# A graph layer's edge sort: the bucket numbers of a comparison are read from PSUM, beside the counts

## The chip, the core and the metric

The kernel runs on one core of a Trainium2 chip. The metric is the device time of one launch in microseconds (us). The engines are named as in the profile: PE (matrix products; PEld is its loading of weights), DVE (vector operations), ACT (activations and copies), POOL (here the issue of indirect DMAs), SP (the queue of most plain DMAs).

## What is computed

A residual graph layer over 12500 nodes of 64 features and 212500 edges (100000 drawn pairs in both directions and one loop for each node). The edges are sorted by `dst`, and `src` is the node that the sums go to.

```python
h = jnp.maximum(_layernorm(x, axis=-1), 0.0)
edge_in = jnp.concatenate([h[row], h[col], dist], axis=1)     # row = src, col = dst
e = jax.nn.silu(edge_in @ eW1 + eb1)
e = jax.nn.silu(e @ eW2 + eb2)
agg = jax.ops.segment_sum(e, row, num_segments=h.shape[0])
node_in = jnp.concatenate([h, agg], axis=1)
out = jax.nn.silu(node_in @ nW1 + nb1) @ nW2 + nb2
x + out
```

## The kernel before

Node `n` belongs to bucket `n mod 100` (`NB` = 100 buckets of `L` = 125 nodes). The kernel writes each edge's half-finished row (the part of the first layer that comes from `dst` and from the distance, 128 numbers, and 16 copies of the edge's place in its bucket) into a table `q` in DRAM, into the bucket of its `src`, at a rank that it counts itself. Then it reads buckets back and finishes the edges there: the `src` part, SiLU, the second product, SiLU, and a product with a 0/1 matrix that sums by node into `aggT`. A last part computes the nodes' output.

*The sorting half* goes by blocks of 1024 edges (`BLK`), 208 blocks, each as 8 tiles of 128 edges (`TB` = 8). `count(s)` finds the ranks of block `s` in three steps, each up to a `yield`:

- On DVE, `oh` (line 352) compares the numbers 1 to 100 with the bucket numbers of the block's edges, `buckets`, a slice of `bkE`: 8 x 100 results on each partition. `each` (line 360) sums `oh` over the 8 tiles. For every second block, `pick` (line 364) builds the selection matrix of the pair of blocks.
- On PE, two products add to the running counts `full`, which stay in PSUM through all blocks: `rest` with the `each` of the block before (line 369), then `before` with the `each` of this block (line 387). Where a level of buckets closes, DVE reads `full` between them (`u`, line 380, and a few more).
- On DVE, `mine` (line 402) multiplies `oh` with `full`, `rank` (line 404) sums it, and `to` (line 406) makes the row numbers. `to` has four buffers.

`send(s)` multiplies the `pick` of a block with its window of rows (PE, `qp`, line 427), copies the results to `qs` (ACT, lines 437 and 443; eight buffers), and issues eight indirect DMAs from POOL (line 450), one for each tile of 128 edges. Each scatters 128 rows of 144 numbers to the rows of `q` that a column of `to` names. `send_all` runs `send(s)` beside `count(s + 1)`, step by step, so on PE the `qp` products of a block stand ahead of the two counting products of the next block, which stand together.

*The finishing half* goes by batches of a level and four buckets, in 450 steps of four tiles: `lr`, `oneT`, `pt`, `e1`, `one`, `p2`, `e2`, `seg`, `aggT` (lines 526 to 603). Its inputs are `qt`, a stretch of `q`, and `a`. It starts while the sorting half still runs: a level of buckets can be read as soon as all edges that can fall into it have been sent.

The order of the work on PE, DVE, ACT and SP is the order in which the program is written (the kernel sets it by hand). A list `turn` gives the order of the finishing steps, with four places in it at which a piece of the sorting half goes in; `marks` says how many pieces must have gone by each step. The semaphores are set by the framework from the tiles that instructions read and write.

In PSUM the pool `sg` holds `full` and the sums `seg` of a batch; the pool `mm` holds four tiles that all other products share, and `p2` two.

Of the kernel before, what the change touches and what calls it, by code (L numbers as in the profile page):

```python
# [28 lines left out]
F32 = mybir.dt.float32  # L29
# [9 lines left out]
P = 128  # L39
# [9 lines left out]
TB = BLK // P  # L49
# [24 lines left out]
def tile_gnn(ctx: ExitStack, tc: tile.TileContext, x, src, dst, ew, eW1, eb1, eW2, eb2, nW1, nb1, nW2, nb2, out):  # L74
    nc = tc.nc
# [4 lines left out]
    NB = N // L  # L80
# [61 lines left out]
    nodes1 = const.tile([P, L], F32, name="nodes1")  # L142
# [126 lines left out]
    with ExitStack() as work:  # L269
        mm = work.enter_context(tc.tile_pool(name="mm", bufs=4, space=PSUM))  # L270
        p2p = work.enter_context(tc.tile_pool(name="p2", bufs=2, space=PSUM))
        sgp = work.enter_context(tc.tile_pool(name="sg", bufs=1, space=PSUM))
# [2 lines left out]
                engines={mybir.EngineType.PE, mybir.EngineType.DVE, mybir.EngineType.Activation, mybir.EngineType.SP}  # L275
            )
        )
        full = sgp.tile([P, NB], F32, name="full")
        nc.tensor.matmul(full, before, identb[:, :NB], start=True, stop=True)
        nc.vector.memset(full, -1.0)  # L280
        mine = cnt.tile([P, TB, NB], F32, name="mine")
        sums = []
        blk, lists = {}, {}
# [43 lines left out]
        def weights(s):  # L327

            if s < nblocks:
                p, g = s // 2, s % 2  # L330
                pick = lists[p][1][:, g]
                e0 = s * BLK
                m = 1 if p == 0 or e0 + 2 * BLK > E else 2
                if m == 2 or e0 + BLK <= E:
                    of = bass.AP(tensor=ew.tensor, offset=ew.offset + e0, ap=[[QR, NQR], [BLK, m], [1, QR]])
                    nc.sync.dma_start(lists[p][1][WL::32, g : g + m, :], of)
                else:
                    for a in range(NQR):
                        m = min(QR, E - e0 - a * QR)
                        if m > 0:  # L340
                            of = bass.AP(tensor=ew.tensor, offset=ew.offset + e0 + a * QR, ap=[[m, 1], [1, m]])
                            nc.sync.dma_start(pick[a * 32 + WL : a * 32 + WL + 1, :m], of)

        def count(s):

            if s < nblocks:
                bc, win, pick = blk[s]
                p, g = s // 2, s % 2
                whole = p > 0 and (2 * p + 2) * BLK <= E
                buckets = bkE[:, g * TB : (g + 1) * TB, p]  # L350
                oh = wk.tile([P, TB, NB], BF16, name="oh")
                nc.vector.tensor_tensor(  # L352
                    oh,
                    nodes1[:, None, :NB].to_broadcast([P, TB, NB]),
                    buckets[:, :, None].to_broadcast([P, TB, NB]),
                    op=OP.is_equal,
                )
                each = wk.tile([P, NB], BF16, name="each")
                with nc.allow_low_precision("whole numbers up to eight"):
                    nc.vector.tensor_reduce(each, oh.rearrange("p t b -> p b t"), AX.X, OP.add)  # L360
                if not whole:
                    nc.vector.tensor_scalar(pick, bc, same, plus, op0=OP.is_equal, op1=OP.add)
                elif g == 0:
                    nc.vector.tensor_scalar(lists[p][1], lists[p][0], same, plus, op0=OP.is_equal, op1=OP.add)
            yield
            if s < nblocks and (g == 0 or not whole):
                weights(s)
            if s > 0:
                nc.tensor.matmul(full, rest, sums.pop(), start=False, stop=True, skip_group_check=True)
            limits = [(SURE[w], OP.is_gt) for w in ready_at if s == ready_at[w]]  # L370
            closed = s > 0 and (s == nblocks or needed[s] != needed[s - 1])
            if closed:
                limits.append((SURE[needed[s - 1]], OP.is_lt))
            if s == nblocks:
                limits.append((ROWS, OP.is_gt))
            if limits:
                u = wk.tile([P, NB], F32, name="u")
                v = wk.tile([P, 1], F32, name="v")
            for limit, op in limits:
                nc.vector.tensor_scalar(u, full, float(G * limit - 1), None, op0=op)  # L380
                nc.vector.tensor_reduce(v, u, AX.X, OP.max)
                nc.vector.tensor_tensor(bad[:, 1:2], bad[:, 1:2], v, op=OP.add)
            if s == nblocks:
                return
            if closed and LEVELS[needed[s - 1]][2]:
                nc.vector.tensor_scalar(full, full, float(G * ENDS[needed[s - 1]] - 1), None, op0=OP.max)
            nc.tensor.matmul(full, before, each, start=False, stop=True, skip_group_check=True)  # L387
            sums.append(each)
            if g == 0:
                assert p in scaled  # L390
                both = bkE[:, :, p].rearrange("p (g t) -> p g t", g=2)
                wide = [P, 2, TB, TB]
                eq = wk.tile(wide, F32, name="eq")
                nc.vector.tensor_tensor(
                    eq, both[:, :, :, None].to_broadcast(wide), both[:, :, None, :].to_broadcast(wide), op=OP.is_equal
                )
                nc.vector.tensor_tensor(eq, eq, early[:, None].to_broadcast(wide), op=OP.mult)
                pre = wk.tile([P, 2 * TB], F32, name="pre")
                nc.vector.tensor_reduce(pre.rearrange("p (g t) -> p g t", g=2), eq, AX.X, OP.add)
                nc.vector.tensor_tensor(offE[:, :, p], offE[:, :, p], pre, op=OP.add)  # L400
            yield
            nc.vector.tensor_tensor(mine, oh, full[:, None, :].to_broadcast([P, TB, NB]), op=OP.mult)  # L402
            rank = wk.tile([P, TB], F32, name="rank")
            nc.vector.tensor_reduce(rank, mine, AX.X, OP.add)  # L404
            to = top.tile([P, TB], I32, name="to")
            nc.vector.scalar_tensor_tensor(  # L406
                to, rank, float(G * ROWS - 1), offE[:, g * TB : (g + 1) * TB, p], op0=OP.min, op1=OP.add
            )
            blk[s].append(to)
            yield  # L410
# [60 lines left out]
        def send_all(s0, s1):  # L471

            for s in range(s0, s1):
                load(s + 2)
                i, rest = divmod(s - FILL0, FILL_EACH)
                if rest == 0 and 0 <= i < len(fills):
                    fill(*fills[i])

                for j, _ in enumerate(itertools.zip_longest(send(s), count(s + 1))):
                    pending[needed[s]] -= j == PIECES - 1  # L480
                    yield
# [329 lines left out]
        with tc.tile_pool(name="lists", bufs=1, side="right") as lp:  # L811
# [40 lines left out]
            list(scale(0, FIRST))  # L852
            load(0)
            counting = count(0)
            next(counting)
            todo = groups()
# [214 lines left out]
```

## Time and profile before

| what | value |
|---|---|
| median of 3 runs | 2500.06 us (2492.88 to 2503.01) |
| profiled execution, its own time | 2495.92 us |
| its span in the trace | 2494.1 us |
| mean granted PE clock | 0.915 |
| PE, DVE, POOL, ACT busy | 82%, 78%, 70%, 44% |
| indirect DMAs of POOL, line 450 | 1661, mean 1030 ns |
| `oh`, line 352 | 208, mean 984 ns |

The page gives the busy time of each engine, the span in 40 slices, the DMA queues, the chain of work that ended last, and the costliest groups of instructions. A group's line has the line of the kernel, the engine, the operation, what it writes and reads, how often it ran, its busy time and mean, and then the idle time of its engine just before it with what ended that idle time. Other views give the waits between engines, the instructions of one line, and the instructions in order of time. Releasers are inferred, and a wait is put down to what came last.

### The profile page before, as it was taken

Reading aid. Unit: us, or ns where it says so; the run is one execution under the profiler, and the core shown is the slowest. Engines: PE = TensorE matmul, PEld = TensorE weight load, DVE = VectorE, ACT = ScalarE, POOL = GpSimd, SP = SyncE. Lnnn points to the kernel's source line nnn. Section 1 sums busy time; section 2 is a strip of 40 time slices with the busy share of each in tenths; the row PEclk is TensorE's granted clock in tenths of the full one; section 3 lists DMA queues with packets and bytes.
Section 4 is the critical chain, followed back from the end, with each engine's and each line's share of the span. In section 5 each row is a group of like instructions: output and inputs, shape, how many; then the busy total and the mean of one; then the engine's idle time right before and its main releaser. Section 6 shows DMA issues by size and latency. Waiting matters only on the chain.

```text
span 2494.1 us, 46291 instructions
## 1 busy us (share of the span) xinstructions
PE 2056.3 (82%) x16191; PEld 1838.5 (74%) x16191; DVE 1936.9 (78%) x3005; ACT 1088.6 (44%) x2403; POOL 1740.7 (70%) x1712
## 2 busy tenths in 40 slices
PE   3663776655588888998889998899999999999997
PEld 2552665555577777887878887788888899999986
DVE  7885677666788887888878888888888899986532
ACT  2451333322244444544444444455455555554442
POOL 4677777777777777777777777777777777762110
PEclk9575888877899998999999999999999999999999
DMA  4563556555667765676645554555555556665652
GB/s 118 182 213 119 168 183 188 179 166 176 194 198 223 222 198 169 219 222 206 202 152 165 164 164 150 165 165 178 166 168 173 179 167 201 216 205 171 194 164 66
DMA packets 237007, 443.85 MB, mean 178 GB/s; under 512 B 49805, under 2 KB 108736, under 8 KB 236562
## 3 DMA queue, kind: packets, MB, share of 16 engines
q1 hardware_dynamic: 158629, 269.79, 35.4%
q0 software_dynamic: 53536, 123.03, 14.2%
q10 hardware_dynamic: 24602, 47.98, 6.6%
q8 instruction: 132, 2.16, 0.4%
q14 instruction: 108, 0.88, 0.1%
HBM read 251.07 MB, written 189.55 MB: 177 GB/s over the span
## 4 chain that ended last, share of the span: by engine, by line
PE 39%; DMA 17%; POOL 14%; DVE 13%; issue 8%; ACT 2%; SPq 0%; DVEq 0%; POOLq 0%; ACTq 0%
DMA q<-qs,to 15%; POOL q L450 14%; PE seg L592 9%; PE pt L546 8%; PE p L578 7%; PE pt L540 4%; PE qp L427 4%; PE lr L526 2%; DVE oh L352 2%; DVE oneT L531 2%; DVE each L360 2%; DVE one L559 2%; DVE aggT L603 2%; DMA qt<-q 1%; DVE mine L402 1%
## 5 line engine op out<-in xcount | busy, mean ns | idle before, releaser
L450 POOL DMA_INDIRECT q<-qs,to x1661 | 1711.6, 1030 | 586.1 <-issue 402.2
L550 ACT ACTIVATE e<-pt 128x512 f32<-128x512 f32 x450 | 268.7, 597 | 867.4 <-PE pt L546 865.2
L592 PE MATMUL seg<-one,e 128*128 128x125 f32 x3600 | 510.3, 287 | 119.0 <-DVE aggT L603 83.7
L592 PEld LDWEIGHTS seg<-one,e 128*128 128x128 f32 x3600 | 462.1, 201 | 170.0 <-issue 110.8
L578 PEld LDWEIGHTS p<-w,e 128*128 128x128 f32 x3600 | 472.0, 196 | 54.2 <-issue 37.3
L546 PE MATMUL pt<-oneT,a 125*128 125x128 f32 (+1 forms) x2400 | 486.8, 337 | 20.0 <-DVE oneT L531 20.0
L578 PE MATMUL p<-w,e 128*128 128x128 f32 x3600 | 494.1, 281 | 0.0
L546 PEld LDWEIGHTS pt<-oneT,a 125*128 125x128 f32 x2400 | 366.3, 199 | 40.6 <-DVE oneT L531 23.1
L437 ACT COPY qs<-qp 128x512 f32<-128x512 f32 x416 | 224.7, 588 | 370.9 <-PE qp L427 321.9
L531 DVE TENSOR_SCALAR oneT<-lr,part 125x512 f32<-125x512 f32 x450 | 335.0, 745 | 48.8 <-PE lr L526 46.8
L360 DVE TENSOR_REDUCE each<-oh 128x100 bf16<-128x800 bf16 x208 | 315.8, 1518 | 7.2
L559 DVE TENSOR_TENSOR one<-nodes,qt 128x500 f32<-128x500 f32 x450 | 302.3, 672 | 0.0
L540 PE MATMUL pt<-ident,qt 128*128 128x128 f32 x1800 | 288.3, 285 | 1.3 <-DVE oneT L531 1.3
L427 PE MATMUL qp<-win,pick 64*128 64x256 f32 x1662 | 270.5, 440 | 22.5 <-DMA win<-tb 6.1
L582 ACT ACTIVATE e<-p 128x512 f32<-128x512 f32 x450 | 268.6, 597 | 27.9 <-PE p L578 27.6
L572 ACT COPY p<-b2f 128x512 f32<-128x512 f32 x450 | 267.2, 594 | 0.0
L406 DVE SCALAR_TENSOR_TENSOR to<-rank,offE 128x8 int32<-128x8 f32 x208 | 36.2, 174 | 280.0 <-DMA q<-qs,to 274.8
L427 PEld LDWEIGHTS qp<-win,pick 64*128 64x128 f32 x1662 | 165.4, 206 | 98.5 <-issue 63.0
L540 PEld LDWEIGHTS pt<-ident,qt 128*128 128x128 f32 x1800 | 201.8, 148 | 48.7 <-issue 38.8
L603 DVE TENSOR_TENSOR aggT<-aggT,seg 128x500 f32<-128x500 f32 x275 | 184.0, 669 | 67.8 <-PE seg L592 64.3
L404 DVE TENSOR_REDUCE rank<-mine 128x8 f32<-128x800 f32 x208 | 205.1, 986 | 7.2
L402 DVE TENSOR_TENSOR mine<-oh,full 128x800 f32<-128x800 bf16 x208 | 203.8, 980 | 6.8 <-PE full L387 6.6
(144 smaller groups left out, 1457.0 us busy)
## 6 DMA issues: line engine op xcount, KB each, us to landing
qt<-q SPq DMA_DIRECT2D x150, 576.0 KB
a<-ta SPq DMA_DIRECT2D x300, 256.0 KB
qt<-q SPq DMA_DIRECT2D x150, 288.0 KB
q<-zeros ACTq DMA_DIRECT2D x25, 1080.0 KB
q<-qs,to POOLq DMA_INDIRECT x1661
q<-zeros ACTq DMA_DIRECT2D x10, 1440.0 KB
bc<-dests SPq DMA_DIRECT2D x103, 128.0 KB
win<-tb SPq DMA_DIRECT2D x416, 30.0 KB
```

The costliest lines, as they stand in the source:

```text
L360: nc.vector.tensor_reduce(each, oh.rearrange("p t b -> p b t"), AX.X, OP.add)
L427: nc.tensor.matmul(qps[i][:, t, : n_of[t]], pick[at, t * P : (t + 1) * P], win[at, : n_of[t]], start=True, stop=True)
L450: ins = nc.gpsimd.indirect_dma_start(out=q[:], out_offset=bass.IndirectOffsetOnAxis(ap=to[:k, j : j + 1], axis=0), in_=qs[:k, t, a, :], in ...
L531: nc.vector.tensor_scalar(oneT, st[k].pop("lr")[:L], part1[:L, :], None, op0=OP.is_equal)
L540: nc.tensor.matmul(pt[:, t, :], qt[:, j, :H], ident, is_transpose=True, start=t == 0, stop=False, skip_group_check=True)
L546: nc.tensor.matmul(pt[:, cols, :], a[:L, b, :], oneT[:, cols, :], start=False, stop=True, skip_group_check=True)
L550: nc.scalar.activation(e1, pt, AF.Silu)
L559: nc.vector.tensor_tensor(one.rearrange("p (b j) l -> p b j l", j=n), nodes1[:, None, None, :].to_broadcast(wide), loc[:, tiles[0][1] : ti ...
L572: nc.scalar.copy(p2, b2f)
L578: nc.tensor.matmul(p2[:, t, :], e1[:, t, :], w2, start=False, stop=t == G - 1, skip_group_check=True)
L582: nc.scalar.activation(e2, p2, AF.Silu)
L592: nc.tensor.matmul(item[2][:, b, :], e2[:, t, :], one[:, t, :], start=j < G, stop=j >= G * (n - 1))
```

## The change

The PSUM tile `full` becomes the first 100 columns of a tile `counts` of 200 columns, in the same pool and one bank. A DVE copy writes the numbers 1 to 100 into the other 100 columns, once, before the first block. `oh` reads these numbers as its first input in place of `nodes1` in SBUF; its second input, `buckets`, stays in SBUF, and its output stays bf16 in SBUF. `nodes1` itself stays, since `one` and the set-up read it.

```diff
-        full = sgp.tile([P, NB], F32, name="full")
+        counts = sgp.tile([P, 2 * NB], F32, name="counts")
+        full, numbers = counts[:, :NB], counts[:, NB:]
         nc.tensor.matmul(full, before, identb[:, :NB], start=True, stop=True)
         nc.vector.memset(full, -1.0)
+        nc.vector.tensor_copy(numbers, nodes1[:, :NB])
         mine = cnt.tile([P, TB, NB], F32, name="mine")
...
                 oh = wk.tile([P, TB, NB], BF16, name="oh")
                 nc.vector.tensor_tensor(
                     oh,
-                    nodes1[:, None, :NB].to_broadcast([P, TB, NB]),
+                    numbers[:, None, :].to_broadcast([P, TB, NB]),
                     buckets[:, :, None].to_broadcast([P, TB, NB]),
                     op=OP.is_equal,
                 )
```

In the built program the order of instructions is the same on every engine, but for the new copy and its neighbour in the set-up on DVE.

## Prediction

> **What bounds the kernel now.** I read the page first (busy times, the chain), then the scatter's own line with its waits, then a stretch of the timeline, then a table of stretches. The page's engine totals mislead: PE is busiest over the span, yet for most of it nothing waits for PE alone.
>
> ```profile
> PE 2056.3 (82%) x16191; PEld 1838.5 (74%) x16191; DVE 1936.9 (78%) x3005; ACT 1088.6 (44%) x2403; POOL 1740.7 (70%) x1712
> ...
> PE 39%; DMA 17%; POOL 14%; DVE 13%; issue 8%; ACT 2%; SPq 0%; DVEq 0%; POOLq 0%; ACTq 0%
> DMA q<-qs,to 15%; POOL q L450 14%; PE seg L592 9%; PE pt L546 8%; PE p L578 7%; PE pt L540 4%; PE qp L427 4%; PE lr L526 2%; DVE oh L352 2%; DVE oneT L531 2%; DVE each L360 2%; DVE one L559 2%; DVE aggT L603 2%; DMA qt<-q 1%; DVE mine L402 1%
> ```
>
> The chain is split between PE and the indirect scatters of POOL (line 450), with their landings. Now line 450 alone: its durations, what POOL waited for, and who waited for it.
>
> ```profile
> L450 POOL DMA_INDIRECT q<-qs,to x1661: 898/967/2278, 39.3 to 2314.1; - x185
> ...
>   issue: 402.2, 1317
> ...
>   DVE to L406: 274.8, 92
>   ACT qs L437: 48.9, 16
> ```
>
> Between 100 and 2240 us of the trace this line is busy 1649.5 us and idle before itself 489.4 us: 2138.9 of 2140. The idle part is a fixed 0.305 us ahead of each of its 1603 scatters; whatever name stands on such a gap, its length is the same. So POOL is full for 2140 us, and DVE waits for it (274.8 us at `to`, whose four buffers are still being scattered). The rows show `to` ready 25 to 30 us ahead of the block's first scatter in nearly all of it. In this stretch the time is POOL's time, one scatter every 0.967 + 0.305 = 1.272 us plus what lengthens some of them.
>
> What lengthens them is in the timeline:
>
> ```profile
> 1200.11 0.98 DVE L352 TENSOR_TENSOR oh<-nodes,bkE 128x800 bf16<-128x800 f32 x1
> ...
> 1200.51 1.43 POOL L450 DMA_INDIRECT q<-qs,to  x1 [0.30 <-issue]
> ...
> 1204.39 0.97 DVE L402 TENSOR_TENSOR mine<-oh,full 128x800 f32<-128x800 bf16 x1
> ...
> 1204.79 0.97 POOL L450 DMA_INDIRECT q<-qs,to  x1 [0.30 <-issue]
> ```
>
> Both scatters start 0.40 us into a DVE instruction of 800 elements. Under `oh`, whose two inputs are both in SBUF, the scatter takes 1.43 us and ends 0.84 us after `oh` does; under `mine`, with `full` in PSUM, it takes its usual 0.97. All rows say the same: of the scatters that reach their 0.13th us inside an `oh`, 128 of 142 are lengthened; inside `one` (two SBUF inputs) 110 of 136; inside `mine` 2 of 150; inside `oneT` (from PSUM) 0 of 249; inside `aggT` (one PSUM input) 0 of 79. The lengthening is 105 us in all; scatters that end 0.84 us after an `oh` carry 54.8 us of it (124 scatters), after a `one` 33.3 us (123), after an `eq` 6.9 us (47).
>
> Last, where POOL stops being the only bound:
>
> ```profile
> 1600.00:2000.00 400.00, 375.79 (x3057) 340.34 (x3056) 348.68 (x527) 204.15 (x436) 308.24 (x302) 0.99 0.53 172
> 2000.00:2240.00 240.00, 233.99 (x2121) 220.89 (x2120) 219.06 (x339) 125.33 (x264) 183.90 (x178) 1.00 0.64 199
> 2240.00:2494.00 254.00, 237.28 (x2028) 216.78 (x2026) 117.16 (x197) 104.72 (x213) 38.65 (x46) 0.98 0.49 150
> ```
>
> Columns: stretch, length, busy PE, PEld, DVE, ACT, POOL, clock, DMA share, GB/s. PE is at 94% up to 2000 us, 97.5% up to 2240, and alone after that.
>
> **The change, part by part.** *Set-up*: a DVE copy of 100 elements joins once; the like-sized `u` took 258 ns. Before the first scatter at 39.3 us DVE is a chain, so 0 to 0.3 us; I take 0.2.
>
> *DVE time of `oh`*: 208 instructions of 984 ns. With one input in PSUM the nearest rows are `mine`, same 800 elements, 980 ns, and `aggT` from PSUM, 669 ns, beside `one` from SBUF, 672 ns, both of 500. So 208 x (-4 to 0 ns) = -0.8 to 0 us, off the path while DVE waits for POOL: 0. [...]
>
> *The wait on the counts' bank*: since `oh` now reads the tile that PE's counting products write, the product with `rest` (line 369) waits for the `oh` of the block; in the built program's order 176 of these 208 products carry a DVE wait, against 49 before. Behind it on PE stand the product with `before`, then the `pt`, `p`, `seg` of the running batch. But the very next product, with `before`, already waits for `each` (141.4 us over 45 waits), which DVE runs directly after `oh` for 1.52 us. The `rest` product takes 0.22 us and lies wholly inside that: nothing is later. The cover is gone only if `each` ended less than 0.22 us after `oh`; then a block would pay up to 0.22 + 0.33 us (the issue gap seen ahead of line 369), 208 x 0.55 = 114 us of PE, of which only the 23 blocks after 2000 us, 13 us, are on the path. In the other direction `oh` carries no wait for PE, since the `mine` ahead of it on DVE has already waited for the same product. DVE's order is otherwise unchanged. I take 0, range 0 to 13.
>
> *POOL*: with the numbers in PSUM, `oh` has one SBUF input left, as `mine` has, and its 54.8 us go. Part comes back: a scatter held by `oh` restarts in step with DVE, and so misses the next `one` more often. Compare blocks: the 122 with a scatter held by `oh` lose 128 ns to other instructions, the 78 without lose 376. If every block went over to the second kind, 122 x 0.248 = 30 us would return, the upper bound; the lower is 0. For a value I walked along the recorded DVE rows with one scatter every 1.272 us, held when it starts more than 0.02 us after the start of a two-SBUF instruction and over 0.13 us before its end. The walk, restarted at each block's recorded scatter, gives 55 for `oh`, 35 for `one`, 96 in all, near the rows' 54.8, 33.3 and 105; with `oh` struck out `one` costs 47 and the sum is 53. So 12 us return, and POOL's stretch gets 43 us shorter (25 to 55).
>
> *Who is late next*: PE. Before 2000 us lie 88% of the stretch, 38 us; PE's 94% there becomes 96%, under the 97.5% that it reaches later, so I let them through. After 2000 PE has 6 us idle in 240; of the 5 us due there I count 1. The tail after 2240 us is PE's alone: 0. Sum: 38 + 1 - 0.2 = 39 us. The profiled execution was 2495.92 us (span 2494.1), so 2457 for its like; it lies 4 us under the median of 2500.06, and from the median it is 2461.
>
> **Rivals.** *The order of operands decides.* `oh` reads PSUM as its first input and SBUF (`buckets`) as its second; `mine` and `aggT` have it the other way round, and no row shows this order while POOL scatters. If the second input is what shuts POOL out, nothing changes: 2500, 2495 to 2505. That is the case in which the change does not do what it says. For it speaks only this gap; against it, that all rows with one PSUM input are clean. [...]
>
> *Freed, but taken up.* The upper give-back (30 us) together with a PE that cannot go past its 94% before 2000 us: 55 - 30 = 25 us of which the 20% that lie after 1600 us are lost, 20 us; with `eq` caught more too, 5 to 20. Time 2480 to 2495. For: PE is at 94% there. Against: 97.5% a little later.
>
> [...]
>
> **How the numbers follow.** The forecast 0.73, range 2443 (all 55 us) to 2478; freed but taken up 0.10; no change 0.12; slower 0.05. About 0.5%, 12.5 us, is what a measurement of this kernel can tell from no change. The forecast is wholly past that; the second case mostly (0.07 of its 0.10). Faster 0.80, same 0.15, slower 0.05. The range for 8 in 10 runs from 2443 to 2492, taking in nearly all of the first two cases.
>
> **What would show it.** Right: the scatters that end 0.84 us after an `oh` are gone, line 450's mean falls from 1030 ns to about 1004, `one` holds more than now, POOL's last scatter comes near 2275 instead of 2315 us, the waits of `to` on scatters shrink, PE between 1600 and 2000 us rises past 95%. Wrong: scatters of 1.4 us under `oh` still there (operand order), PE waits at line 369's successor with DVE long done (the bank), or an `oh` over 1.02 us.

## Result and the profile after

The changed kernel took 2463.94 us in the median of 4 runs (2459.37 to 2467.58), the kernel before 2499.5 us in its 4. The ratio is 0.986 with a 95% interval of 0.9832 to 0.9888: 36 us, or 1.4%, faster. The profiled execution took 2461.70 us (span 2459.9).

First the page after: the busy times and the chain.

```profile
PE 2045.2 (83%) x16191; PEld 1829.8 (74%) x16191; DVE 1936.9 (79%) x3006; ACT 1088.8 (44%) x2403; POOL 1705.5 (69%) x1712
...
PE 36%; DMA 17%; DVE 16%; POOL 13%; issue 8%; ACT 2%; DVEq 0%; POOLq 0%; ACTq 0%; SPq 0%
```

DVE is as busy as before to 0.1 us; POOL is busy 35 us less for the same 1661 scatters. Now the groups of instructions: the scatter's line, and the two counting products on PE. First before, then after.

```profile
L450 POOL DMA_INDIRECT q<-qs,to x1661 | 1711.6, 1030 | 586.1 <-issue 402.2 <-ACT qs L443 84.0 <-DMA q<-qs,to 42.4
...
L369 PE MATMUL full<-each,rest 128*128 128x100 bf16 x208 | 46.6, 224 | 0.6 <-DVE mine L402 0.6
L387 PE MATMUL full<-each,before 128*128 128x100 bf16 x208 | 45.4, 218 | 174.0 <-DVE each L360 141.4 <-DVE u L380 22.2 <-DVE full L386 10.3
```

```profile
L452 POOL DMA_INDIRECT q<-qs,to x1661 | 1676.4, 1009 | 586.3 <-issue 396.9 <-ACT qs L445 85.4 <-DMA q<-qs,to 43.7
...
L371 PE MATMUL counts<-each,rest 128*128 128x100 bf16 x208 | 46.5, 224 | 92.0 <-DVE oh L354 92.0
L389 PE MATMUL counts<-each,before 128*128 128x100 bf16 x208 | 45.1, 217 | 73.2 <-DVE each L362 48.8 <-DVE u L382 13.9 <-DVE counts L388 10.2
```

The mean scatter went from 1030 to 1009 ns (the prediction's sign was about 1004), while the idle time ahead of the scatters stayed (586.1 and 586.3 us). The new wait is there, 92.0 us at the product with `rest`, and the old one at the product with `before` has shrunk to 73.2; before, they were 0.6 and 174.0.

The timeline after has a scatter that starts 0.38 us into an `oh`, and a little later one that starts 0.41 us into a `one`.

```profile
369.20 0.98 DVE L354 TENSOR_TENSOR oh<-counts,bkE 128x800 bf16<-128x800 f32 x1
369.58 0.97 POOL L452 DMA_INDIRECT q<-qs,to  x1 [0.31 <-issue]
...
374.52 0.67 DVE L561 TENSOR_TENSOR one<-nodes,qt 128x500 f32<-128x500 f32 x1
374.93 1.11 POOL L452 DMA_INDIRECT q<-qs,to  x1 [0.31 <-issue]
```

Under `oh` the scatter now takes its usual 0.97 us; under `one`, still with two inputs in SBUF, it is held and takes 1.11. Over all rows: scatters that start inside an `oh` (0.02 us after its start to 0.15 us before its end) were held in 124 cases of 125 before, and in 0 of 114 now.

Last, the stretches that answer to those of before (length, busy PE, PEld, DVE, ACT, POOL, clock, DMA share, GB/s).

```profile
1600.00:1970.00 370.00, 352.45 (x2906) 320.39 (x2905) 327.93 (x500) 194.53 (x416) 284.28 (x282) 1.00 0.54 175
1970.00:2205.00 235.00, 229.45 (x2081) 216.73 (x2080) 215.04 (x331) 122.05 (x257) 178.74 (x175) 1.00 0.65 198
2205.00:2460.00 255.00, 237.85 (x2032) 217.31 (x2031) 117.43 (x198) 105.18 (x213) 38.66 (x46) 0.98 0.50 150
```

PE went from 94% to 95.3% in the first stretch and from 97.5% to 97.6% in the second. POOL is full up to about 2210 us now instead of 2245; the stretch behind it is as long as it was.

### The profile page after: what moved, and what is told of

It is laid out like the page before. It is cut to its first block, busy times and chain, and to the rows that moved or that the text cites. A ratio compares the mean times of both kernels' runs of the same rounds, so it can differ in the third digit from the quotient of the medians.

```text
span 2459.9 us, 46292 instructions
## 1 busy us (share of the span) xinstructions
PE 2045.2 (83%) x16191; PEld 1829.8 (74%) x16191; DVE 1936.9 (79%) x3006; ACT 1088.8 (44%) x2403; POOL 1705.5 (69%) x1712
## 4 chain that ended last, share of the span: by engine, by line
PE 36%; DMA 17%; DVE 16%; POOL 13%; issue 8%; ACT 2%; DVEq 0%; POOLq 0%; ACTq 0%; SPq 0%
DMA q<-qs,to 16%; POOL q L452 13%; PE seg L594 8%; PE pt L548 8%; PE p L580 7%; PE pt L542 4%; PE qp L429 4%; DVE oh L354 2%; DVE each L362 2%; DVE oneT L533 2%; PE lr L528 2%; DVE aggT L605 2%; DVE one L561 2%; DVE mine L404 1%; DVE rank L406 1%
## 5 line engine op out<-in xcount | busy, mean ns | idle before, releaser
L452 POOL DMA_INDIRECT q<-qs,to x1661 | 1676.4, 1009 | 586.3 <-issue 396.9
L594 PE MATMUL seg<-one,e 128*128 128x125 f32 x3600 | 504.0, 285 | 110.2 <-DVE aggT L605 77.7
L594 PEld LDWEIGHTS seg<-one,e 128*128 128x128 f32 x3600 | 456.0, 199 | 140.0 <-issue 84.7
L404 DVE TENSOR_TENSOR mine<-oh,counts 128x800 f32<-128x800 bf16 x208 | 203.9, 980 | 8.3 <-PE counts L389 8.0
```

Of the source, the lines that this page charges most:

```text
L452: ins = nc.gpsimd.indirect_dma_start(out=q[:], out_offset=bass.IndirectOffsetOnAxis(ap=to[:k, j : j + 1], axis=0), in_=qs[:k, t, a, :], in ...
L594: nc.tensor.matmul(item[2][:, b, :], e2[:, t, :], one[:, t, :], start=j < G, stop=j >= G * (n - 1))
```

## Experiments

The theory: POOL's scatters set the time; a scatter that starts inside a DVE instruction with two SBUF inputs is held (inside `oh` before, 124 of 125), so that it ends 0.84 us after that instruction does; the change takes `oh` off that list, and the time falls by what the scatters then lose less. The rivals were the order of the operands, a price of the new wait, and a PE that takes the gain up. All results stand together first. "Lengthened" is the time of all scatters over 0.968 us each, "idle" what POOL idled between scatters over the fixed 0.306 us, both from the rows of the profiled execution; "rest" is the span less the end of the last scatter.

Each ratio is against runs of the kernel before made beside that kernel (their medians were 2499.5 us for the second row, 2497.4 for the next four, 2496.7 for the last two), so it is not quite the quotient of the medians shown.

| kernel | median us | ratio to before | lengthened | of it `oh` / `mine` / `one` | idle | last scatter ends | rest |
|---|---|---|---|---|---|---|---|
| before | 2499.5 | 1 | 106.0 | 54.8 / 0 / 33.3 | 58.0 | 2315.0 | 179.1 |
| changed | 2463.9 | 0.986 | 71.0 | 0 / 0 / 46.5 | 58.1 | 2280.2 | 179.7 |
| inputs of `oh` exchanged | 2464.1 | 0.9863 | 72.5 | 0 / 0 / 46.7 | 59.8 | 2283.2 | 179.2 |
| wait alone | 2499.8 | 1.0003 | 109.3 | 50.0 / 0 / 41.3 | 61.1 | 2321.4 | 179.6 |
| `oh` and `one` from PSUM | 2421.7 | 0.9695 | 15.4 | 0 / 0 / 0 | 74.4 | 2240.2 | 178.8 |
| `mine` from an SBUF copy | 2551.4 | 1.0226 | 130.4 | 0 / 54.1 / 56.7 | 86.8 | 2367.9 | 178.8 |
| copy, `mine` from PSUM | 2518.5 | 1.0097 | 67.4 | 0 / 0 / 43.6 | 119.0 | 2336.9 | 178.8 |
| `one` alone from PSUM | 2468.2 | 0.9895 | 68.3 | 54.8 / 0 / 0 | 68.2 | 2287.0 | 178.8 |

Take "lengthened" and "idle" from the end of the last scatter and 2150 to 2151 us are left in all eight kernels. That by itself is bookkeeping: 1661 scatters of 0.968 us, 1660 gaps of 0.306 us and a first scatter at 39 us make 2155, less some 4 us of scatters and gaps that are a little shorter. What the runs add is that the 179 us behind the last scatter stay, so that the time moves with two sums alone: the lengthening and POOL's idle time. A kernel wins only what it takes off the first and does not add to the second.

**The order of the inputs.** The changed kernel, with the two inputs of `oh` exchanged.

```diff
-                    numbers[:, None, :].to_broadcast([P, TB, NB]),
                     buckets[:, :, None].to_broadcast([P, TB, NB]),
+                    numbers[:, None, :].to_broadcast([P, TB, NB]),
```

> Theory (what shuts POOL out is the number of inputs in SBUF, not their order): with the two inputs of oh exchanged, bucket numbers first from SBUF and the numbers 1 to 100 second from PSUM, the time stays at that of the changed kernel, 2464 us within 6, and no scatter ends 0.84 us after an oh; PSUM as the first input was clean in the changed kernel, PSUM as the second was clean in mine. Rival (some of the gain hangs on PSUM being first): scatters held by oh come back, up to 55 us of them, and the time goes to 2475 to 2500.

Ratio 0.9863 (0.9844 to 0.9883), and 0 of the 106 scatters that start inside an `oh` are held. With PSUM as the first input (0 of 114) as with PSUM as the second, `oh` leaves the scatters alone. This rival falls, by the changed kernel itself and by this one.

**The wait alone.** The kernel before, with the product with `rest` waiting for `oh`.

```diff
-                nc.vector.tensor_tensor(
+                compared = nc.vector.tensor_tensor(
...
-                nc.tensor.matmul(full, rest, sums.pop(), start=False, stop=True, skip_group_check=True)
+                ins = nc.tensor.matmul(full, rest, sums.pop(), start=False, stop=True, skip_group_check=True).ins
+                if s < nblocks:
+                    tc.add_manual_dep(ins, compared.ins.name, AFTER)
```

> The kernel before, with one thing of the change alone: the product with rest waits for the oh of its block, as it does in the changed kernel; the numbers stay in SBUF. Theory (the wait lies inside the wait for each that follows): 2500 us within 5, the idle time of PE moves from the product with before to the product with rest and their sum stays near 164 us (174 us of PE idle before line 387 now, 10 of it at a closing level). Rival (the product with rest now comes after the wait and PE pays 0.22 to 0.55 us a block): 13 us or more above the kernel before, 2513 to 2525, and the changed kernel would have won as much more without the wait.

Ratio 1.0003 (0.9993 to 1.0012, 11 runs): at most 3 us. The groups of this kernel:

```profile
L369 PE MATMUL full<-each,rest 128*128 128x100 bf16 x208 | 47.2, 227 | 99.5 <-DVE oh L352 99.5
L389 PE MATMUL full<-each,before 128*128 128x100 bf16 x208 | 45.5, 219 | 76.0 <-DVE each L360 52.5 <-DVE u L382 12.7 <-DVE full L388 10.5
```

99.5 and 76.0 us make 175.5, against 0.6 and 174.0 before: the idle time moved from one product to the other. The wait costs nothing here, because the second product has to wait for `each` anyway.

**More of the same.** The changed kernel, with the numbers 1 to 125 for `one` in the same bank.

```diff
-        counts = sgp.tile([P, 2 * NB], F32, name="counts")
-        full, numbers = counts[:, :NB], counts[:, NB:]
+        counts = sgp.tile([P, NB + L], F32, name="counts")
+        full, numbers, all_numbers = counts[:, :NB], counts[:, NB : 2 * NB], counts[:, NB:]
...
-        nc.vector.tensor_copy(numbers, nodes1[:, :NB])
+        nc.vector.tensor_copy(all_numbers, nodes1)
...
-                nodes1[:, None, None, :].to_broadcast(wide),
+                all_numbers[:, None, None, :].to_broadcast(wide),
```

> The changed kernel, with the numbers 1 to 125 of one in the bank of the counts too. Theory (POOL's scatters are the bound until PE is): the 46 us that scatters lose to one go, 5 to 15 of them come back at eq and pick, POOL's last scatter is 30 to 40 us earlier, at 2240 to 2250; PE, at 96% from 1600 us on, lets 10 to 30 us of it through: 2434 to 2454. Rival (PE has become the bound, and one now waits for the counting product and the counting product for one): POOL's scatters run 0.97 us each but wait, the time is 2460 to 2490.

2421.7 us, ratio 0.9695 (0.9679 to 0.971): the fastest kernel of the study, 76 us under the kernel before of the same runs. The last scatter came where it was expected, at 2240 us, though not by the steps expected, and the time beat the expected range. Nothing came back at `eq` and `pick`: the lengthening fell by 55.6 us, 46.5 of them at `one`. Against that POOL idled 16.3 us more, most of it from 2112 us on, and it waited for `qs` 99.8 us instead of 85.4. So about 16 of the 56 us were taken up by POOL's waits, and the other 40 came off the end. PE was busy 96.6% of the time between 1600 and 2150 us. It idled longer at the product with `rest`, which now waits for `one` too (141.1 us); whether this wait is part of the 16 us was not tested.

```profile
L452 POOL DMA_INDIRECT q<-qs,to x1661 | 1620.4, 976 | 602.6 <-issue 396.8 <-ACT qs L445 99.8 <-DMA q<-qs,to 40.7
```

**The cost put back elsewhere.** The changed kernel, with `mine` reading a copy of the counts in SBUF.

```diff
+            held = wk.tile([P, NB], F32, name="held")
+            nc.scalar.copy(held, full)
-            nc.vector.tensor_tensor(mine, oh, full[:, None, :].to_broadcast([P, TB, NB]), op=OP.mult)
+            nc.vector.tensor_tensor(mine, oh, held[:, None, :].to_broadcast([P, TB, NB]), op=OP.mult)
```

> The changed kernel, with the suspected cost put back at another place: ACT copies the counts to SBUF (208 copies of 100 columns, about 0.3 us each) and mine reads the copy, so mine has two inputs in SBUF and oh has one. Theory: mine holds scatters as oh did, 30 to 55 us of lengthening, less at one than the 46 us now; the time goes to 2485 to 2510. Rival (what held the scatters was particular to oh, such as its place after to, and not its inputs): the time stays within 8 us of 2464, and no scatter ends 0.84 us after a mine.

```profile
489.08 0.98 DVE L406 TENSOR_TENSOR mine<-oh,held 128x800 f32<-128x800 bf16 x1
489.48 1.42 POOL L454 DMA_INDIRECT q<-qs,to  x1 [0.30 <-issue]
```

`mine`, which holds at most 1 scatter in each of the other kernels, now holds scatters just as `oh` did: 126 of the 134 that start inside it, 54.1 us. So it is the place of the inputs and nothing particular to `oh`. ACT's copy took 253 ns in the mean. The time, 2551.4 us, lies 41 us beyond the expected range, and this kernel changed two things, the input and the copy with its wait. So the copy was left in and `mine` put back to PSUM:

```diff
-            nc.scalar.copy(held, full)
-            nc.vector.tensor_tensor(mine, oh, held[:, None, :].to_broadcast([P, TB, NB]), op=OP.mult)
+            copied = nc.scalar.copy(held, full).ins
+            ins = nc.vector.tensor_tensor(mine, oh, full[:, None, :].to_broadcast([P, TB, NB]), op=OP.mult).ins
+            tc.add_manual_dep(ins, copied.name, AFTER)
```

> The kernel with ACT's copy of the counts and mine behind it, mine reading PSUM, once more, since in the runs just made the kernel before took 3049 us. Against a kernel before at 2500 us. Theory (two causes): scatters held by mine are gone, the lengthening of the scatters is about 71 us in all, and the time is 2480 to 2505. Rival (the copy and its wait are all of the 87 us between the changed kernel and the one in which mine reads the copy): near 2551.

2518.5 us, ratio 1.0097 (1.0063 to 1.0131), 13 us over the range: none of the scatters that start inside `mine` is held, but the copy and its wait cost about 55 us against the changed kernel, more than supposed. The waits show where: DVE's `mine` waits for the copy, and POOL waits for `qs` 135.0 us instead of 85.4.

```profile
DVE mine L406 <- ACT held L405: 208.3, 141, 3.7
POOL q L455 <- ACT qs L448: 135.0, 49, 22.0
```

From 1990 us on POOL is no longer full in this kernel. The place of the input alone, the step from this kernel to the one ahead of it, lengthens the scatters by 63 us but the time by only 33, because POOL idles 32 us less: in part the held scatters only filled time in which POOL had waited.

**`one` alone.** The kernel with `oh` and `one` from PSUM, with the numbers of `oh` put back to SBUF.

```diff
-                    numbers[:, None, :].to_broadcast([P, TB, NB]),
+                    nodes1[:, None, :NB].to_broadcast([P, TB, NB]),
```

> The numbers of one from PSUM, those of oh from SBUF, once more, for the same reason. Theory: the 33 us at one go and 2 come back at oh, 31 us won: 2462 to 2475. Rival: the shares simply add up to the 78 us of both, so 2455 to 2460, or the held scatters at oh grow as those at one did, to 70, so 2480 to 2490.

2468.2 us, ratio 0.9895 (0.9863 to 0.9927): in the expected range. The 33 us at `one` went, `oh` stayed at 54.8; in all the lengthening fell by 37.7 us and POOL idled 10.2 more. The two shares do not add: 36 us for `oh` and 28 to 31 for `one` make less than the 76 to 78 of both. The table fits the reason given beforehand: `one` catches 13 us more once `oh` is clean, and only a clean `one` gets those back.

The last two kernels had been run once before, with the same code:

> The last kernel with its copy of the counts by ACT, and mine waiting for that copy, but mine reads the counts from PSUM again: what is left between the two is only where the second input of mine lies. Theory (two causes in that kernel: 54 us of scatters held by mine and 10 more at one, and about 30 us from the copy, through which DVE comes late at the end of POOL's stretch): scatters held by mine are gone, line 450's scatters are lengthened by about 71 us in all as in the changed kernel, and the time is 2480 to 2505. Rival (the copy and its wait are the whole of the 87 us): the time stays near 2551.

> The numbers of one from PSUM, those of oh from SBUF again. Theory (each instruction's share is what its held scatters cost, less what others then catch): the 33 us at one go; the walk along the rows of the kernel before gives 57 at oh in place of 55, so 31 us are won: 2462 to 2475. Together with the 36 us of the change alone this is less than the 78 us of both, since the 13 us that came back at one are then gone too. Rival (the shares simply add, or the held scatters at oh grow as those at one did, to 70): 2455 to 2460, or 2480 to 2490.

There the kernel before itself took 3049 us, so nothing can be read from their 3099 and 3079 us about a kernel of 2500. In the profiles of the two kernels 10% and 12% of the chain are put down to another core or an unknown queue. POOL idled about 700 us there, mostly waiting for `qs` (735.5 and 688.8 us). Scatters were held and freed in the same way (124 of 124 inside the `oh` that reads SBUF were held), but freeing them won nothing: ratios 1.0162 (1.01 to 1.0224) and 1.0114 (1.0051 to 1.0177), both slower than the kernel before. What slowed those runs was not found.

## Why the prediction was right

The forecast was 2461 us, the result 2464, by the mechanism named. Step by step:

- *What bounds*: right. POOL is full until about 2245 us before and 2210 after; from there to the last scatter it waits some 50 us in both kernels, and 179 us follow.
- *`oh` itself*: 983 ns after, 984 before, inside the -4 to 0 ns that the prediction took from the rows of `mine` and `aggT`; exchanged, with PSUM as the second input, it is 980 ns.
- *The wait*: right, nothing, now by an experiment. The 13 us at the upper end were not needed.
- *The 54.8 us at `oh`*: gone to the last scatter. PSUM as the first input, which no row of the kernel before showed while POOL scatters, does what PSUM as the second does: with one SBUF input `oh` holds 0 of 114 scatters in the changed kernel and 0 of 106 with its inputs exchanged. The prediction's list, two SBUF inputs, was too short, though: `pick` has one tensor input, in SBUF, and holds 27 of the 29 scatters that start 0.1 to 0.4 us into it (last section). Why it does, no run here shows.
- *What comes back*: the term that was mis-sized. 12 us were taken, 20 came. `one` rose from 33.3 to 46.5 us, 13 where the walk gave 12. But scatters that end 0.84 us after a `pick` carry 4.0 us where they carried none, and `pick` was not among the instructions that the walk let hold a scatter; another 3 us lie scattered over the set-up and cases with no clear cause.
- *PE*: mis-sized the other way. Four of POOL's 43 us were to be lost to PE after 2000 us; none were. The rest behind the last scatter is 179.1 and 179.7 us. The two errors of 8 and 4 us partly cancel, which is luck: 35 - 0 was measured where 43 - 4 was forecast.
- *Set-up*: the first scatter came 0.4 us later instead of 0.2; over the eight kernels it lies between 39.1 and 39.7 us without a pattern.
- *The range*: its lower end, 2443 for all 55 us, is 2 us lower than 2500 less 55 gives; nothing else rests on it.

Of the rivals, the order of operands (0.9863) and a price of the new wait (1.0003) are refuted by runs of their own. "Taken up" did not occur here: POOL's idle time stayed at 58 us. It began one step later, when `one` was freed too and 16 of the 56 us went into POOL's waits.

## What to carry to other kernels

Look for the engine with no idle time but a fixed gap in a stretch, and not for the busiest over the span: POOL at 70% set this kernel's time, and the 35 us off its scatters came off the end. When a queue of indirect DMAs on POOL is that engine, list the DVE instructions with two inputs in SBUF that run beside it (here `oh` held 124 of 125 scatters), and look at the ones with one input for held scatters too (`pick` held 27 of 29). Here, putting one input, even a constant, into spare columns of a PSUM bank freed the scatters (0 of 114 held), and the bank's new wait cost nothing (ratio 1.0003 with the wait alone) because it fell inside a wait that was there already. Expect to lose part of the gain to the instructions that are still on the list (here 20 of 54.8 us), and with each that you free, watch whether POOL begins to wait: then the next engine takes its share.

## Not expected of the hardware

`pick` has one tensor input, bf16 numbers in SBUF, and yet it holds scatters. Before, none of the 19 scatters that start inside a `pick` was held, so it looked harmless. All 19 had started in its first 0.1 us, and none of them in the 64 blocks in which `oh` held a scatter and a `pick` follows: there one scatter starts about 0.3 us ahead of `pick` and the next after its end. After the change scatters meet it at all phases, and of the 29 that start 0.1 to 0.4 us into it 27 are held, as here:

```profile
349.32 0.54 DVE L366 TENSOR_SCALAR pick<-bc,same,plus 128x512 f32<-128x512 bf16 x1
349.62 1.08 POOL L452 DMA_INDIRECT q<-qs,to  x1 [0.30 <-issue]
```

So a DVE instruction that is clean in a trace can be clean by its phase alone. What sets `pick` apart from the clean instructions was not tested. The rows show one difference, its pace (before):

```profile
L364 DVE TENSOR_SCALAR pick<-bc,same,plus 128x512 f32<-128x512 bf16 x102 | 54.8, 537 | 0.0
...
L362 DVE TENSOR_SCALAR pick<-bc,same,plus 128x256 f32<-128x256 bf16 x4 | 1.6, 403 | 0.0
```

Its 256 further elements take 134 ns, 0.52 ns each; from `one` (500 elements, 672 ns) to `oh` (800, 984 ns) each takes 1.04 ns.

The other surprise is how sharp the rule is: in the kernel before, of 158 scatters that start up to 0.4 us ahead of a `one`, 1 is lengthened; of 102 that start 0.05 to 0.45 us into one, all 102 are, and 99 of them end 0.84 us after the `one` does, the other three 1.16 to 1.18.
